# A reciprocal square root without its Newton step on VectorE, and a row of ones made by ScalarE

## The chip, the cores and the metric

The kernel runs on one core of a Trainium2 chip. The metric is the device time of one execution in microseconds (us). A core has five engines with their own queues: TensorE (PE, with its weight loads shown as PEld), VectorE (DVE), ScalarE (ACT), GpSimd (POOL) and SyncE (SP), which issues the DMA transfers here. Each engine works through its instructions in order and waits for others on semaphores.

## What is computed

Four images of 56 x 56 pixels and 96 channels pass through four layers. Layers 0 and 1 contain a selective scan (a state-space recurrence) in four directions over the image, with 192 inner channels and 16 states; layers 2 and 3 are an attention without softmax, followed by a feed-forward part with quantized weights and activations (fp8 products, fp16 sums). In front of the parts and between them stand normalisations:

```python
def layer_norm(x, w, b, eps=1e-06):
    m = jnp.mean(x, axis=-1, keepdims=True)
    v = jnp.mean((x - m) ** 2, axis=-1, keepdims=True)
    return (x - m) * jax.lax.rsqrt(v + eps) * w + b
...
h = da_t * h + db_t * x_t[..., None]
y_t = jnp.einsum('bds,bs->bd', h, c_t)
```

The attention is linear in its values, so the kernel needs only the Gram matrix of the normalised tokens, each extended by a one (for the biases): a matrix of 97 x 97 per image.

## The kernel before

**The scan.** The two scan layers are one long sequence of rounds: 2 layers x 4 images x 4 directions x 7 chunks of 448 tokens x 2 halves of the channels x 4 groups of states = 1792 rounds. Each round takes three tiles of 128 x 448 (`NG = 3`). `decay` (L640) lets ScalarE compute exp(dt * a) into one PSUM tile `da` for each of the three; `begin` (L645) lets TensorE spread b over the partitions into PSUM (L580); VectorE multiplies du by b (L673), for two of the three tiles, or all three in the rounds in `OWN` and `OWN_TAIL`, where GpSimd does not take the third (L651). VectorE then runs three scans (L699), ScalarE saves and restores the carries (L703, L658), GpSimd multiplies the result by c (L709, `hc`), and TensorE adds up over the states (L737). The parts of the next chunk (softplus, L489 and L490; products on GpSimd, L496 and L593) are woven in at fixed rounds.

**The rest, beside the scan.** The other work runs in lanes beside the scan: `load`, `middle`, `fuse`, `attend`, Python generators that issue one step at a time. The scan loop yields twice a round: once as slot "F", after the multiplies have been issued, and once as slot "C", between the first and the second of the three scans. So what a lane issues in a C slot stands in VectorE's queue between scan 0 and scan 1, and in ScalarE's queue behind the first decay of the next round. A lane's yield names the slot that its next step wants, the PSUM tiles that it holds, and the load in us that it puts on ScalarE (`a`) and TensorE (`p`); `overlap` (L902) and `room` (L940) admit steps by these numbers. Inside the scan the order of the instructions on TensorE, ScalarE, VectorE and GpSimd is that of the calls (`manual_schedule`, L1303). While image i of layer 1 is scanned, image i-1 goes through `fuse` and `attend`; the last image does so in a tail without a scan, after `late` (L191), with more buffers and an order that is left to the scheduler. Before the scan, `load(0)` runs alone; in it `self.tables` is still false.

**The normalisations.** `normed` (L814) centres x by a matmul (`factor`), squares it on ScalarE (L776) and calls `spread_factor` (L779). That averages the squares by four small matmuls into a PSUM tile `ps` of 112 x 4 (L789), turns the variances into 1/sqrt, and spreads the four columns over 96 partitions by four matmuls (L809), whose result VectorE multiplies with x in a later C slot (L823, L1125, L1166; through a copy at L1111 and L1117). The 1/sqrt takes two forms. With `tables` false: a GpSimd power (L794). Otherwise, in the F slot, Ln and Exp(-0.5 x) on ScalarE (L801, L802) give a first value r; in the next C slot three VectorE instructions do one Newton step on it (L804 to L806). `spread_factor` in this second form runs 245 times: 21 in `load`, 56 in `middle`, 84 in `fuse` with the `gram` it calls, and 84 in `attend` with its `gram`.

**The row of ones.** `gram` (L1216) takes a tile `xra` of 97 x 448, one of three buffers inside the scan (`depth`) and of six in the tail, fills row 96 with ones (L1220), lets `normed` write rows 0 to 95, stores these by DMA (L1222), transposes all 97 rows on TensorE (L1226) and adds up the Gram matrix. It is called 56 times, 28 from `fuse` and 28 from `attend`. The row is issued in the C slot (or behind a yield of C) from which `gram` is entered.

Of the kernel before, what the change touches and what calls it, by code (L numbers as in the profile page):

```python
# [11 lines left out]
F32 = mybir.dt.float32  # L12
# [3 lines left out]
AF = mybir.ActivationFunctionType  # L16
ALU = mybir.AluOpType
# [5 lines left out]
C = 96  # L23
# [5 lines left out]
NT = 112  # L29
CW = 448  # L30
# [134 lines left out]
class Net:  # L165
# [613 lines left out]
    def spread_factor(self, eps, *terms):  # L779

        nc = self.nc
        ps = self.ps()
        blocks = [slice(q * NT, (q + 1) * NT) for q in range(4)]
        for q, b in enumerate(blocks):
            for n, (sq, avg) in enumerate(terms):
                nc.tensor.matmul(ps[:NT, q : q + 1], sq[:, b], avg, start=n == 0, stop=n == len(terms) - 1)  # L789
        rs = self.wp.tile([NT, 4], F32, name="rs", bufs=12)  # L790
        if not self.tables:
            yield "F0 a.3"
            nc.scalar.activation(rs, ps[:NT, :4], AF.Identity, bias=self.eps[eps][:NT])
            nc.gpsimd.tensor_tensor(rs, rs, self.power[:NT], ALU.pow)  # L794
            yield "C1 p2.4"
        else:

            yield "F1 a.6"

            r, t = self.wp.tile([NT, 4], F32, name="rs", bufs=12), ps[:NT, 4:8]  # L800
            nc.scalar.activation(r, ps[:NT, :4], AF.Ln, bias=self.eps[eps][:NT])  # L801
            nc.scalar.activation(r, r, AF.Exp, scale=-0.5)  # L802
            yield "C1 p2.4"
            nc.vector.scalar_tensor_tensor(t, ps[:NT, :4], eps, r, ALU.add, ALU.mult)  # L804
            nc.vector.scalar_tensor_tensor(t, t, -0.5, r, ALU.mult, ALU.mult)
            nc.vector.scalar_tensor_tensor(rs, t, 1.5, r, ALU.add, ALU.mult)  # L806
        ps = self.ps()[:C, :CW]
        for q, b in enumerate(blocks):
            nc.tensor.matmul(  # L809
                ps[:, b], rs[:, q : q + 1].to_broadcast([NT, C]), self.ident[:NT, :NT], start=True, stop=True  # L810
            )
        return ps
# [403 lines left out]
    def gram(self, n, i, c, x, s):  # L1216

        nc = self.nc
        xr = self.wp.tile([C + 1, CW], F32, name="xra", bufs=self.depth)
        nc.vector.memset(xr[C : C + 1], 1.0)  # L1220
        yield from self.normed(1e-5, x, 1, xr[:C])
        nc.sync.dma_start(self.xrd[i][:, s], xr[:C])  # L1222
        m = C + 1
        ps = self.ps()
        for q in range(4):
            nc.tensor.transpose(ps[:NT, q * m : (q + 1) * m], xr[:, q * NT : (q + 1) * NT], self.ident[:m, :m])  # L1226
        yield "F0 a.5"
        t = self.w()
        nc.scalar.copy(t[:NT, : 4 * m], ps[:NT, : 4 * m])
        yield "C1 p2.4"  # L1230
        ps = self.ps()[:m, :m]
        for q in range(4):
            a = t[:NT, q * m : (q + 1) * m]
            nc.tensor.matmul(ps, a, a, start=q == 0, stop=q == 3)
        yield "C0"
        if c == 0:
            self.g[i] = self.wp.tile([m, m], F32, name="gram", bufs=3)
            nc.vector.tensor_copy(self.g[i], ps)
        else:
            nc.vector.tensor_tensor(self.g[i], self.g[i], ps, ALU.add)  # L1240
# [98 lines left out]
```

## Time and profile before

Three runs took 8621.33, 8633.8 and 8647.61 us, median 8633.8 us. The profiled execution has a span of 8626.1 us and a mean granted TensorE clock of 0.892.

| engine | busy us | share of the span | instructions |
|---|---|---|---|
| DVE | 7939.4 | 92% | 10933 |
| POOL | 7594.3 | 88% | 4075 |
| PE | 7475.5 | 87% | 33459 |
| ACT | 5909.3 | 69% | 12541 |

| group | count | busy us | mean ns |
|---|---|---|---|
| L699 DVE scans | 5376 | 5523.8 | 1072 |
| L673 DVE multiplies | 4172 | 2330.0 | 605 |
| L709 POOL multiply by c | 1792 | 5168.2 | 2885 |
| L651 POOL third multiply | 1204 | 1374.6 | 1142 |
| L643 ACT decays | 5376 | 3394.5 | 633 |
| L804 / L805 / L806 DVE, with `ps` as their PSUM tile | 215 each | 34.4 / 36.6 / 34.7 | 160 / 170 / 161 |
| L1220 DVE memset of the row | 56 | 24.2 | 432 |

A group's busy time is the union of its instructions, its mean the length of one; where instructions overlap, the two differ. The remaining 30 of the 245 Newton steps have their PSUM tile in `da`, `y`, `b` or `pp`, in the tail. Busy shares over the whole span mix three stages: up to about 119 us the lead-in, up to 8286 us the scan, then the tail.

### The profile page before, as it was taken

How to read it: one execution, taken by the hardware profiler on the slowest of the kernel's cores; microseconds unless marked ns; L12 is line 12 of the kernel's file. 1: busy time of each engine (PE TensorE's matmuls, PEld its weight loads, DVE VectorE, ACT ScalarE, POOL GpSimd, SP SyncE). 2: the span in 40 equal slices, each digit the busy share in tenths (PEclk: the TensorE clock that was granted, in tenths of full speed). 3: DMA queues.
4: the chain of work that ended last, by engine and by line, in shares of the span. 5: the costliest groups of instructions: out<-in, count | busy, mean ns of one | idle time of the engine just before them, and what ended most of it. 6: DMA issues, size and time to landing. Idle time of an engine off the chain costs nothing. (4 is left out here: it accounts for less than half of the span.)

```text
span 8626.1 us, 120872 instructions
## 1 busy us (share of the span) xinstructions
PE 7475.5 (87%) x33459; PEld 2708.0 (31%) x33459; DVE 7939.4 (92%) x10933; ACT 5909.3 (69%) x12541; POOL 7594.3 (88%) x4075
## 2 busy tenths in 40 slices
PE   6788888898889888898889989988899888998997
PEld 3222223232333223232223223323233232333345
DVE  5999999999999999999999999999999999999951
ACT  5777667676777667776677756667766777667646
POOL 4888989999999999999999999999999999999940
PEclk8888889898999989998899989988899888998987
DMA  5677677677777777776777777667776677766731
GB/s 144 159 184 174 164 179 179 162 167 166 187 169 179 168 185 173 172 176 159 185 175 171 170 174 166 161 154 167 185 174 150 161 165 186 171 149 163 168 90 45
DMA packets 951340, 1417.89 MB, mean 164 GB/s; under 512 B 176578, under 2 KB 943812, under 8 KB 949796
## 3 DMA queue, kind: packets, MB, share of 16 engines
q1 hardware_dynamic: 949888, 1408.37, 68.6%
q8 instruction: 263, 4.31, 0.2%
q14 instruction: 417, 3.42, 0.2%
q10 hardware_dynamic: 772, 1.80, 0.1%
HBM read 1141.42 MB, written 268.14 MB: 163 GB/s over the span
## 5 line engine op out<-in xcount | busy, mean ns | idle before, releaser
L709 POOL TENSOR_TENSOR hc<-v,cb 128x1344 f32<-128x1344 f32 x1792 | 5168.2, 2885 | 499.4 <-DVE v L699 288.1
L699 DVE TENSOR_TENSOR_SCAN v<-da,v 128x449 f32<-128x449 f32 (+1 forms) x5376 | 5523.8, 1072 | 60.4 <-ACT v L658 33.2
L643 ACT ACTIVATE da<-dt,na 128x448 f32<-128x448 f32 x5376 | 3394.5, 633 | 1583.2 <-DVE v L699 1557.3
L673 DVE TENSOR_TENSOR v<-du,b 128x448 f32<-128x448 f32 x4172 | 2330.0, 605 | 136.5 <-PE b L580 50.0
L737 PE MATMUL y<-hc,four 128*32 128x448 f32 x14336 | 1959.6, 622 | 4.3 <-POOL hc L709 4.3
L580 PE MATMUL b<-cf,sel 128*128 128x448 bf16 x1792 | 682.6, 381 | 954.7 <-DVE v L673 949.9
L651 POOL TENSOR_TENSOR v<-du,cb 128x448 f32<-128x448 f32 x1204 | 1374.6, 1142 | 95.8 <-DMA cb<-cd 69.0
L724 PE MATMUL y<-w,zeros 128*96 128x448 bf16 x5117 | 1441.9, 399 | 0.0
L724 PEld LDWEIGHTS <-zeros 128*96 128x96 bf16 x5117 | 631.5, 134 | 1306.5 <-issue 1149.6
L737 PEld LDWEIGHTS y<-hc,four 128*32 128x32 f32 x14336 | 297.5, 114 | 1291.2 <-issue 917.7
L428 PE MATMUL pp<-U,wd 96*128 96x448 f32 x896 | 671.3, 836 | 9.1 <-DMA U<-u 9.1
L733 PE MATMUL y<-Y,ident 96*96 96x448 f32 x672 | 539.8, 892 | 42.3 <-ACT Y L744 23.6
L496 POOL TENSOR_TENSOR duc<-dtc,U 96x448 f32<-96x448 f32 x448 | 559.8, 1250 | 4.6 <-ACT dtc L490 4.6
L886 PE MATMUL ps<-win,dg 64*64 64x220 f32 (+9 forms) x1962 | 509.3, 454 | 0.0
L703 ACT COPY carry<-v 128x3 f32<-128x3 f32 x1536 | 299.2, 195 | 287.7 <-DVE v L699 286.9
L480 PE MATMUL pp<-cf,wd 12*96 12x448 f32 (+1 forms) x896 | 488.0, 627 | 1.1 <-ACT cf L467 1.0
L489 ACT ACTIVATE dtc<-pp,wd 96x448 f32<-96x448 f32 x448 | 279.3, 623 | 270.1 <-PE pp L480 267.7
L593 POOL TENSOR_TENSOR cf<-cf 64x448 f32<-64x448 f32 x448 | 417.5, 932 | 35.7 <-ACT cf L467 0.6
L744 ACT COPY Y<-y 96x448 f32<-96x448 f32 x448 | 339.3, 757 | 31.8 <-PE y L737 30.6
L886 PEld LDWEIGHTS ps<-win,dg 64*64 64x64 f32 (+2 forms) x1962 | 230.6, 158 | 329.9 <-issue 272.7
L580 PEld LDWEIGHTS <-sel 128*128 128x128 bf16 x1792 | 186.7, 104 | 350.2 <-issue 285.8
L733 PEld LDWEIGHTS y<-Y,ident 96*96 96x96 f32 x672 | 116.8, 184 | 553.2 <-ACT da L643 243.8
(426 smaller groups left out, 6066.0 us busy)
## 6 DMA issues: line engine op xcount, KB each, us to landing
cb<-cd SPq DMA_DIRECT2D x3584, 112.0 KB, 4.3
dt<-dd SPq DMA_DIRECT2D x1792, 168.0 KB, 4.4
du<-dd SPq DMA_DIRECT2D x1792, 168.0 KB, 4.2
dd<-dtc SPq DMA_DIRECT2D x448, 168.0 KB, 2.0
dd<-duc SPq DMA_DIRECT2D x448, 168.0 KB, 2.1
U<-u SPq DMA_DIRECT2D x112, 168.0 KB, 4.6
z<-w SPq DMA_DIRECT2D x56, 224.0 KB, 3.1
u<-w SPq DMA_DIRECT2D x56, 224.0 KB, 3.4
```

Source lines behind the costliest of these rows:

```text
L428: self.nc.tensor.matmul(ch.ps.rearrange("p (a b) -> p a b", b=HS), ch.par.wx[:, e], self.in_order(self.U[e], ch.orient, ch.c * CS, CS), st ...
L496: self.nc.gpsimd.tensor_tensor(du.rearrange("p (a b) -> p a b", b=HS), ch.dtc[e].rearrange("p (a b) -> p a b", b=HS), self.in_order(self.U ...
L580: self.nc.tensor.matmul(ps, self.sel[:, q], self.upper(ch.cf), start=True, stop=True)
L643: nc.scalar.activation(da[g][:, TOKENS], ch.dt[e][:, g], AF.Exp, scale=ch.par.na[:, e, q, g : g + 1])
L651: nc.gpsimd.tensor_tensor(v[:, 2, TOKENS], ch.du[e][:, 2], ch.cb[q][:, 1], ALU.mult)
L673: nc.vector.tensor_tensor(v[:, g, TOKENS], ch.du[e][:, g], b, ALU.mult)
L699: nc.vector.tensor_tensor_scan(v[:, g, way], da[g][:, way], v[:, g, way], 0.0, ALU.mult, ALU.add)
L709: nc.gpsimd.tensor_tensor(hc, v[:, :, TOKENS], ch.cb[q][:, 0].unsqueeze(1).to_broadcast([128, NG, CS]), ALU.mult)
L724: self.nc.tensor.matmul(self.y[:C], self.zeros, self.some, start=False, stop=False)
L733: nc.tensor.matmul(o, w, self.in_order(a, ch.orient, ch.c * CS, CS), start=True, stop=False)
L737: nc.tensor.matmul(self.y[32 * n : 32 * n + 32], self.four, hc[:, g], start=n == 3, stop=n == 3 or q == NQ - 1,)
L886: self.nc.tensor.matmul(o[:, a - r0 : e - r0, x0:x1], diag[:, tap], win[:, a + dy - lo : e + dy - lo, x0 + dx : x1 + dx], start=n == 0, st ...
```

## The change

Two edits.

The Newton step goes. Ln and Exp now write straight into `rs`, the tile that the broadcast matmuls read; the second tile r and the spare columns of the PSUM tile are not used any more. This drops three small VectorE instructions per use. Only the form with `tables` true is touched.

The row of ones in `gram` is made by ScalarE: an activation Copy with scale 0 and bias 1 of a column of the identity matrix, broadcast over 448 elements, takes the place of a VectorE memset. It stands at the same point of the program. The numbers in the yields stay as they are.

```diff
             yield "F1 a.6"
-
-            r, t = self.wp.tile([NT, 4], F32, name="rs", bufs=12), ps[:NT, 4:8]
-            nc.scalar.activation(r, ps[:NT, :4], AF.Ln, bias=self.eps[eps][:NT])
-            nc.scalar.activation(r, r, AF.Exp, scale=-0.5)
+            nc.scalar.activation(rs, ps[:NT, :4], AF.Ln, bias=self.eps[eps][:NT])
+            nc.scalar.activation(rs, rs, AF.Exp, scale=-0.5)
             yield "C1 p2.4"
-            nc.vector.scalar_tensor_tensor(t, ps[:NT, :4], eps, r, ALU.add, ALU.mult)
-            nc.vector.scalar_tensor_tensor(t, t, -0.5, r, ALU.mult, ALU.mult)
-            nc.vector.scalar_tensor_tensor(rs, t, 1.5, r, ALU.add, ALU.mult)
...
         xr = self.wp.tile([C + 1, CW], F32, name="xra", bufs=self.depth)
-        nc.vector.memset(xr[C : C + 1], 1.0)
+        nc.scalar.activation(xr[C:], self.ident[C : C + 1, :1].to_broadcast([1, CW]), AF.Copy, scale=0.0, bias=1.0)
         yield from self.normed(1e-5, x, 1, xr[:C])
```

## The prediction

> **What bounds the kernel now.** I first cut the span into its stages with the busy time of each engine per stretch: a lead-in up to 119 us, eight passes of the scan of about 1021 us each (119 to 8286 us, two layers by four images), and a tail of 340 us. The rows are passes 0, 3 and 6; columns after the length are PE, PEld, DVE, ACT, POOL busy, granted PE clock, DMA share.
>
> ```profile
> core 0: us, PE busy (x) PEld busy (x) DVE busy (x) ACT busy (x) POOL busy (x), PEclk, DMA share, GB/s
> 119.00:1140.00 1021.00, 836.60 (x3624) 281.19 (x3624) 957.14 (x1274) 727.84 (x1486) 903.74 (x470) 0.86 0.71 170
> ...
> 3182.00:4203.00 1021.00, 881.30 (x3932) 297.76 (x3933) 988.18 (x1303) 718.05 (x1469) 953.94 (x505) 0.91 0.74 175
> ...
> 6245.00:7265.00 1020.00, 911.18 (x4190) 335.46 (x4189) 982.74 (x1387) 704.31 (x1591) 951.78 (x518) 0.90 0.70 166
> ...
> sum 8167.00, PE 7108.32 PEld 2484.96 DVE 7847.36 ACT 5686.54 POOL 7553.74; mean PE 888.54 PEld 310.62 DVE 980.92 ACT 710.82 POOL 944.22
> ```
>
> DVE is busy 7847 of 8167 us (96%), POOL 92%, PE 87%, ACT 70%. So who waits for whom decides. These are rows of the view of waits for passes 5 to 7 (5224 to 8286 us); the figures are us in total, times, longest.
>
> ```profile
> DVE ps L804 <- ACT rs L802: 42.9, 53, 2.4
> DVE w L1100 <- ACT w L776: 8.8, 7, 3.9
> ...
> POOL hc L709 <- DVE v L699: 103.9, 126, 4.6
> ...
> PE b L580 <- DVE v L673: 270.3, 272, 2.7
> ...
> ACT da L643 <- DVE v L699: 542.0, 710, 2.7
> ```
>
> POOL, PE and ACT all wait for DVE; DVE itself waits for little, and its longest wait in these passes is that of the first Newton instruction (L804) for Exp on ACT (L802). DVE sets the end of the scan, POOL is close behind. The tail has DVE busy 72 of 340 us; its chain runs over PE and ACT.
>
> Third, DVE in order of time, to see what the edited lines cost where they stand (start us, length us). Scan instructions (L699) without anything between them start (3.05 - 1.08)/2 = 0.985 us apart.
>
> ```profile
> 5311.19 0.17 DVE L804 SCALAR_TENSOR_TENSOR ps<-ps,rs 112x4 f32<-112x4 f32 x1 [0.22 <-ACT rs L802]
> ...
> 5328.76 1.08 DVE L699 TENSOR_TENSOR_SCAN v<-da,v 128x449 f32<-128x449 f32 x1
> 5329.76 0.15 DVE L804 SCALAR_TENSOR_TENSOR ps<-ps,rs 112x4 f32<-112x4 f32 x1
> 5329.94 0.17 DVE L805 SCALAR_TENSOR_TENSOR ps<-ps,rs 112x4 f32<-112x4 f32 x1
> 5330.15 0.16 DVE L806 SCALAR_TENSOR_TENSOR rs<-ps,rs 112x4 f32<-112x4 f32 x1
> 5330.23 1.08 DVE L699 TENSOR_TENSOR_SCAN v<-da,v 128x449 f32<-128x449 f32 x1
> ...
> 5338.86 3.05 DVE L699 TENSOR_TENSOR_SCAN v<-da,v 128x449 f32<-128x449 f32 x3
> ...
> 5342.87 1.08 DVE L699 TENSOR_TENSOR_SCAN v<-da,v 128x449 f32<-128x449 f32 x1
> 5344.10 0.43 DVE L1220 MEMSET xra<- 1x448 f32 x1
> 5344.56 1.09 DVE L699 TENSOR_TENSOR_SCAN v<-da,v 128x449 f32<-128x449 f32 x1
> ```
>
> A Newton trio pushes the next scan from 0.985 to 1.47 us: it costs 0.485 us without a wait. A memset of the row pushes it to 1.69 us: 0.705 us, though it is listed with 0.43 us, since it starts 0.25 us late.
>
> **What the Trainium skill says.** "VectorE: DVE Perf Modes", section "Two Vector instructions with no wait between them": an instruction whose output starts in another quadrant than the last output into the same memory waits until all earlier Vector instructions have finished. The row lies at partition 96, the scan's output at 0. The trace agrees: no overlap ahead of the memset or behind it, 0.705 instead of 0.43 us. "ScalarE: Activation LUTs", section "Table sets: the hidden batching unit": copy is in every set, and Ln and Exp share one. The trace agrees for Copy (the cf copies of L467 have no table load); for Ln and Exp it does from about 320 us on, while the first three uses at L801 and L802 each have a load of 1.28 us. These uses stay, so the number of loads does not change. "SBUF — State Buffer", section "SBUF: two separate sides": DVE and POOL exclude each other only over a shared port pair, used by DVE instructions with two SBUF inputs or in a two-port mode. The trace shows POOL's hc multiply between 2855 and 2948 ns over the whole run, beside any DVE work, so I expect no change in POOL's durations.
>
> **The change, part by part.**
> *Newton trios.* 245 run, 205 of them in the scan: 21 in pass 0, 56 in passes 1 to 4, 128 in passes 5 to 7. 205 x 0.485 = 99 us of DVE. With them goes DVE's wait for L802: 73.7 us in the scan (42.9 in passes 5 to 7, about 7 in 1 to 4, 23.6 in pass 0).
> *Memsets.* 44 in the scan, all in passes 5 to 7: 44 x 0.705 = 31 us of DVE.
> *What DVE gains*: 99 + 74 + 31 = 204 us: 136 in passes 5 to 7 (62 + 43 + 31), 34 in passes 1 to 4 (27 + 7), 34 in pass 0 (10 + 24).
> *The wait that moves.* The broadcast matmuls (L809) now wait for ACT's Exp itself instead of the trio. Behind them on PE stand the y sums and the next b spread (L580), which DVE needs. PE waited for the trio only 3.5 us in passes 5 to 7, and Exp ends before the trio did, so PE starts earlier: cost nothing. The PSUM tile comes free at Ln instead of at L806, also earlier.
> *The row on ACT.* No 1x448 activation is in the trace. Nearest row: SBUF to SBUF, 96x448, L490, 577 ns; the page on ScalarE, section "What ACT_TABLE_LOAD costs", prices immediate scale and bias at 186 ns + 0.833 ns per element, which I estimate as 559 ns; the bottom is the pitch of PSUM copies, 0.42 us. I take 0.56: 44 x 0.56 = 25 us of ACT in the scan. It is queued in the C slot, behind the first decay (L643) and its carry copy, ahead of the second decay. DVE needs that second decay after two more scans, two multiplies and a scan, 2.0 + 1.1 + 1.0 = 4.1 us; ACT needs 0.64 + 0.18 + 0.56 + 0.63 = 2.0 us. Hidden, if ACT is not already late. The row's buffer is one of three, and the memset had to wait for its release 1.5 us in all, once; ACT inherits that.
> *What the others take back.* In passes 5 to 7 POOL waits only 104 us for DVE's scans, less than the 136 us DVE gains. Once that is used up POOL gates, and POOL and DVE are coupled by three v buffers. PE has 270 us and is not first. I take some 90% of the 104: 95 us. In passes 1 to 4 POOL and PE have room (POOL waits over 20 us per pass for scans): 29 of 34. In pass 0 the three L804 waits with table loads in them make 8.9 us; after the one at 275 us ACT still has two loads to do before the decay that DVE needs at 280.0, so that one is not won, and PE runs at 0.86 clock: 22 of 34. Scan: 95 + 29 + 22 = 146 us.
> *Tail.* 40 trios leave a DVE that is idle four fifths of the time; a trio lies on the chain at 8543.56 to 8544.14, 0.6 us, so perhaps 2 to 5 us are won, while 12 rows add 12 x 0.56 = 7 us to ACT, half of it hidden. I put zero, plus or minus 10, since the order of the tail is not written by hand.
> Sum: 8634 - 146 = 8488 us.
>
> **Rivals.**
> 1. *DVE's whole gain comes through* (0.08): POOL's other waits (on y sums, on L809: 38 us in passes 5 to 7) shrink too. For: those stand behind PE work that starts earlier now. Against: POOL would be busy 98% there. 8634 - 204 - 5 = 8425.
> 2. *POOL and PE become the bound in passes 5 to 7* (0.18): coupling through three buffers and more DVE waits for b leave a third of the gain there, 45, and 35 in the others. For: POOL's multiplies come in groups in rounds 5 to 7 of a chunk, where POOL has no idle time. Against: in rounds with a trio POOL waits for DVE up to 1.3 us. 8634 - 80 = 8554.
> 3. *ACT becomes the gate, slower than before* (0.06): ACT waits in order for the row's buffer, and the decays stand behind it. If each of 44 rows cost a round of about 4.55 us plus 0.56, that is 225 us against the 204 won: 8634 + 21 = 8655. For: DVE waited for ACT at L804 53 times there, so ACT does run late. Against: the buffer was free in all cases but one, and ACT idles 542 us on scans in these passes.
> 4. *No difference* (0.04): the freed time becomes waits for b, since PE takes a lower granted clock. PE at 911 of 1020 us would need 0.90 to fall to 0.84.
>
> **How the numbers follow.** My forecast has 0.64. The range 8425 to 8570 holds it with its spread (8450 to 8525), rival 1 and rival 2 with some 16 us of scatter; what lies outside is rivals 3 and 4 and the edges. Within 0.3% is 8608 to 8660. Faster: 0.64 + 0.08 + 0.18 = 0.90; same 0.05; slower 0.05 (rival 3 lies near the border and is shared between the two).
>
> **What would show it.** DVE busy in the scan falls by about 130 us (205 trios, 44 memsets), with no row for L804 to L806; DVE's list of waits has no L804, and no other row grows by more than some 20 us. POOL's wait for scans in passes 5 to 7 falls from 104 to about 20 and its share rises above 96%. Pass 6 is about 32 us shorter, passes 1 to 4 about 7 each. L809 waits for ACT rs by a few us. ACT shows 56 short rows of 0.4 to 0.6 us, and a wait there for DMA or PE stays under 5 us. I am wrong if DVE's waits for b, v of POOL, or da grow by tens of us, if the granted clock falls, or if ACT is seen waiting at the row.

## The result, and the profile after

The changed kernel takes 8486.6 us in the median, against 8640.7 us for the kernel before in the same comparison: a ratio of 0.9828, 95% interval 0.98 to 0.9855 (about 24 us either way). The forecast was 8488 us.

The profiled execution after has a span of 8506.0 us; it is the slowest of those timed, some 20 us above the median, so stage lengths read from it give away some of the gain. The busy time of each engine by stage (passes 0 to 4, passes 5 to 7, tail; the borders between passes are taken at the start of the same instruction, L463, in both kernels; columns as in the prediction), first before, then after:

```profile
core 0: us, PE busy (x) PEld busy (x) DVE busy (x) ACT busy (x) POOL busy (x), PEclk, DMA share, GB/s
118.00:5129.00 5011.00, 4277.77 (x18946) 1438.60 (x18946) 4812.00 (x6343) 3543.11 (x7227) 4621.69 (x2438) 0.90 0.73 172
5129.00:8286.00 3157.00, 2830.55 (x12976) 1046.36 (x12974) 3036.30 (x4284) 2143.59 (x4843) 2932.05 (x1593) 0.90 0.70 166
8286.00:8626.00 340.00, 287.57 (x1293) 177.75 (x1291) 72.12 (x223) 173.42 (x397) 28.02 (x25) 0.78 0.17 47
```

```profile
119.00:5079.00 4960.00, 4260.05 (x18936) 1436.61 (x18936) 4779.47 (x6110) 3536.76 (x7228) 4619.20 (x2438) 0.90 0.73 174
5079.00:8158.00 3079.00, 2801.99 (x12987) 1039.47 (x12985) 2963.04 (x3857) 2162.69 (x4887) 2929.33 (x1593) 0.91 0.71 170
8158.00:8506.00 348.00, 298.86 (x1293) 184.72 (x1291) 48.78 (x91) 179.75 (x409) 27.93 (x25) 0.75 0.17 45
```

The scan lost 51 us in passes 0 to 4 and 78 us in passes 5 to 7; the tail grew by 8. In the scan VectorE's busy time fell by 32.5 + 73.3 = 106 us and its idle time by only 23 us. Yet the wait at L804, 73.7 us, is gone, so about 50 us of idle time are new (more, counting the short gaps around trios and memsets). The view of waits says where in passes 5 to 7 (total us, times, longest), first two rows of before, then after:

```profile
DVE v L673 <- PE b L580: 3.4, 5, 1.7
...
DVE xq L1166 <- PE ps L809: 1.0, 1, 1.0
```

```profile
DVE v L673 <- issue: 18.3, 16, 3.6
DVE w L1095 <- ACT w L776: 17.9, 12, 6.2
DVE v L673 <- PE b L580: 17.9, 20, 2.6
DVE w L1112 <- PE ps L1110: 9.1, 9, 1.8
DVE xq L1161 <- PE ps L804: 9.1, 8, 2.8
DVE v L699 <- POOL v L651: 7.7, 10, 1.9
DVE xra L818 <- PE ps L804: 6.5, 10, 1.9
...
POOL hc L709 <- DVE v L699: 67.4, 70, 5.2
...
PE b L580 <- DVE v L673: 233.2, 219, 3.3
```

Added up by the engine waited for, VectorE's waits in these passes were before: ACT 62, PE 23, POOL 13, without a releaser 5; after: ACT 32, PE 50, POOL 14, without a releaser 18. VectorE's waits for GpSimd did not grow. The rise is at TensorE: the b spread (3.4 to 17.9 us) and the products that read the spread factor (L1161 and L818, before L1166 and L823: 1.7 to 15.6 us). The 13 us more without a releaser stand at the multiplies (L673), and the profile names no cause for them. GpSimd still waits 67 us for scans. In passes 0 to 4 the row that grew most (from 0.4 us) is again a product that reads the spread:

```profile
DVE w L818 <- PE ps L804: 20.0, 14, 3.1
```

One such place, in order of time on VectorE and on TensorE:

```profile
8140.99 1.08 DVE L699 TENSOR_TENSOR_SCAN v<-da,v 128x449 f32<-128x449 f32 x1
8143.59 0.62 DVE L1161 TENSOR_TENSOR xq<-w,ps 96x448 fp8e5<-96x448 f32 x1 [1.52 <-PE ps L804]
8144.13 1.08 DVE L699 TENSOR_TENSOR_SCAN v<-da,v 128x449 f32<-128x449 f32 x1
...
8140.30 2.48 PE L881 MATMUL ps<-win,dg 96*96 96x448 f32 x6
8142.62 0.93 PE L804 MATMUL ps<-ident,rs 112*96 112x112 f32 x8
```

VectorE is ready at 8142.07, but TensorE has a piece of a convolution (L881) ahead of the spread and delivers it at 8143.55. What stands ahead differs from place to place: of the 35.6 us in which VectorE waits for a spread in the scan, 17 us are behind matmuls of other steps beside the scan (L840 and L988), 8 us behind a projection of a later chunk (L428), and a convolution is ahead at this one place only.

The row on ScalarE was estimated at 0.56 us and takes 0.571, and ScalarE never waits at it in the scan:

```profile
L1215 ACT ACTIVATE xra<-ident x44: 571/571/573, 5255.0 to 8080.9; 1x448 f32<-1x448 f32 x44
```

### The profile page after: what moved, and what is told of

Same layout as the page of the kernel before. It is cut to its first block, busy times and chain, and to the rows that moved or that the text cites. A ratio compares the mean times of both kernels' runs of the same rounds, so it can differ in the third digit from the quotient of the medians.

```text
span 8506.0 us, 120303 instructions
## 1 busy us (share of the span) xinstructions
PE 7442.0 (87%) x33459; PEld 2707.3 (32%) x33459; DVE 7810.2 (92%) x10142; ACT 5928.4 (70%) x12597; POOL 7589.0 (89%) x4075
## 5 line engine op out<-in xcount | busy, mean ns | idle before, releaser
L673 DVE TENSOR_TENSOR v<-du,b 128x448 f32<-128x448 f32 x4172 | 2331.4, 605 | 164.7 <-PE b L580 68.4
L737 PE MATMUL y<-hc,four 128*32 128x448 f32 x14336 | 1942.7, 617 | 3.7 <-POOL hc L709 3.6
L428 PE MATMUL pp<-U,wd 96*128 96x448 f32 x896 | 671.2, 836 | 13.7 <-DMA U<-u 13.7
L737 PEld LDWEIGHTS y<-hc,four 128*32 128x32 f32 x14336 | 297.0, 114 | 1206.0 <-issue 816.8
L881 PE MATMUL ps<-win,dg 64*64 64x220 f32 (+9 forms) x1962 | 507.9, 453 | 0.0
L881 PEld LDWEIGHTS ps<-win,dg 64*64 64x64 f32 (+2 forms) x1962 | 229.7, 158 | 326.2 <-issue 267.4
```

What stands on the lines that cost most here:

```text
L428: self.nc.tensor.matmul(ch.ps.rearrange("p (a b) -> p a b", b=HS), ch.par.wx[:, e], self.in_order(self.U[e], ch.orient, ch.c * CS, CS), st ...
L673: nc.vector.tensor_tensor(v[:, g, TOKENS], ch.du[e][:, g], b, ALU.mult)
L737: nc.tensor.matmul(self.y[32 * n : 32 * n + 32], self.four, hc[:, g], start=n == 3, stop=n == 3 or q == NQ - 1,)
L881: self.nc.tensor.matmul(o[:, a - r0 : e - r0, x0:x1], diag[:, tap], win[:, a + dy - lo : e + dy - lo, x0 + dx : x1 + dx], start=n == 0, st ...
```

## Experiments

**The two edits apart.** The Newton step alone is taken away:

```diff
-        nc.scalar.activation(xr[C:], self.ident[C : C + 1, :1].to_broadcast([1, CW]), AF.Copy, scale=0.0, bias=1.0)
+        nc.vector.memset(xr[C : C + 1], 1.0)
```

> The first edit alone: the three Newton instructions are gone, the row of ones stays a VectorE memset. Theory (VectorE sets the end, the parts add up, most of what it gains comes through): the memsets are 44 x 0.705 = 31 us of VectorE in the scan, so this lies 20 to 31 us above the full change, at 8507 to 8518 us. Rival (the row on ScalarE delays the decays as much as the memset cost VectorE): same as the full change, 8487 us, or below.

Measured: 8518.2 us, ratio 0.9867 (0.9852 to 0.9882). As the theory has it: with the step gone, the memsets cost 32 us in the medians (34 by the ratios), against 31 worked out. The interval of the full change overlaps with this one; that of the kernel below in which nobody makes the row, at 8489.5 us, does not.

The row alone moves to ScalarE, with the kernel before otherwise as it was (the reverse edit):

> The second edit alone: the row of ones by ScalarE, the Newton step kept. Theory: 20 to 31 us below the kernel before, 8610 to 8621 us, and no wait of ScalarE at the row. Rival (ScalarE is late in these passes, and the row makes the wait of L804 for Exp longer): 8641 us or more, with the wait at L804 in passes 5 to 7 grown from 43 us.

Measured: 8656.4 us against 8640.1, ratio 1.0026 (1.0014 to 1.0037): slower, as the rival said. The waits of VectorE in passes 5 to 7 (of an execution that took 14 us more than the median):

```profile
DVE ps L804 <- ACT rs L802: 52.9, 57, 2.4
DVE v L673 <- issue: 15.6, 14, 2.5
DVE w L1100 <- ACT w L776: 15.1, 9, 5.6
```

The wait at L804 grew from 42.9 to 52.9 us, the wait for squares at L1100 from 8.8 to 15.1; VectorE's waits for ACT together from 62 to 81. So the same edit is worth 32 to 34 us with the step gone and costs 22 us with it. The next two runs ask which half of the edit does that.

**The row made by nobody.** Three constant tiles take turns inside the scan, and their row 96 is written once; in the tail the row is made as it was. First on the full change:

```diff
+        xra = [const.tile([C + 1, CW], F32, name=f"xra{j}") for j in range(DEPTH)]
+        for t in xra:
+            nc.vector.memset(t[C : C + 1], 1.0)
+        self.xra = cycle(xra)
...
+        if self.ring is None:
+            xr = next(self.xra)
+        else:
+            xr = self.wp.tile([C + 1, CW], F32, name="xra", bufs=self.depth)
```

> The full change, but inside the scan the row of ones is written only once into three constant tiles that take turns, so neither VectorE nor ScalarE makes it there (in the tail ScalarE still does). Theory (the 44 activations of 0.57 us are hidden on ScalarE): same as the full change, 8480 to 8490 us. Rival (they delay the decays and squares that VectorE waits for): up to 25 us below, 8462 us.

Measured: 8489.5 us, ratio 0.9831 (0.9818 to 0.9845), the same as the full change. Without the step the row on ScalarE is hidden, to within the intervals.

The same on the kernel before, Newton step kept:

> The kernel before, its Newton step kept, with the rows of ones written only once inside the scan: the 44 memsets are gone and ScalarE has nothing for them. It tells why moving the row alone was 16 us slower (8656) although it freed 31 us of VectorE. Theory (with the step kept, VectorE waits at L804 for ScalarE, and 0.57 us more on ScalarE come straight back there): 20 to 31 us below the kernel before, 8609 to 8621 us. Rival (as long as VectorE stops at L804 for Exp, what it gains just before is waited out there, whoever makes the row): 8640 to 8656 us.

Measured: 8629.1 against 8635.7 us, ratio 0.9996 (0.9987 to 1.0005), so 31 us less work on VectorE won at most 11. Neither figure was met; it lies between the two, and the wait at the step's first instruction, which has line 808 in this kernel, had grown from 42.9 to 49.5 us, though ScalarE had nothing more to do:

```profile
DVE ps L808 <- ACT rs L806: 49.5, 54, 3.7
DVE w L1104 <- ACT w L780: 15.3, 9, 7.0
```

In this one execution the scan was some 17 us shorter than before and the tail 14 us longer; the tails of the profiled executions lie between 336 and 361 us, the next experiment's apart. So in the scan about half of the 31 us was kept, and how much came back at the step, and how much only in the tail, isn't settled. The six kernels, as the difference to the kernel before (ratio less one, times 8636 us; the intervals are 8 to 13 us either way, for -149 it is 24):

| | row by VectorE | row by nobody | row by ScalarE |
|---|---|---|---|
| step kept | 0 | -3 | +22 |
| step gone | -115 | -146 | -149 |

Reading along the lines: with the step kept, 44 rows of 0.57 us = 25 us on ScalarE show in full (from -3 to +22); with the step gone they show not at all. The explanation that offers itself is that VectorE stops for Exp there, so that ScalarE's lateness becomes its own. It is not shown: between the kernels with the row by nobody and by ScalarE the wait at the step grew only from 49.5 to 52.9 us and the one for squares not at all (15.3 and 15.1), while passes 5 to 7 grew by some 31 us (3140 to 3171). The rest lies in many small waits, the largest part of it (4.1 to 15.6) without a releaser.

**The step later, to take away its wait only.** On the kernel before:

```diff
+            yield "C1"
             yield "C1 p2.4"
             nc.vector.scalar_tensor_tensor(t, ps[:NT, :4], eps, r, ALU.add, ALU.mult)
```

> The kernel before with the Newton step moved one C slot later, so that Exp is long done when VectorE comes to it: the same work, without the wait of 74 us. Theory (the wait costs what it shows): 50 to 74 us below the kernel before, 8567 to 8591 us. Rival (ScalarE and TensorE are late at that point anyway, and VectorE will stand a little further on instead): 8625 to 8641 us, with waits of VectorE for b (L580) or da (L643) grown by tens of us.

Measured: 8693.6 us, ratio 1.0066 (1.0053 to 1.0079): outside both. The wait at L804 was gone from the list, and the scan was 14 us shorter in the profile (its last scan ended at 8272 us against 8286), but the tail took 425 us instead of 340: one more slot in each normalisation made the lanes too long for their passes, and work that belongs beside the scan ran after it (1536 matmuls in the tail instead of 1293). What the wait is worth can't be read from this run, but its profile has the rival's sign: over the scan VectorE's wait for b rose from 50 to 73 us. And it shows that a slot in a lane has a price here.

**The step kept as work, unused.** On the full change, in the same slot, with a constant for r:

```diff
+            d, t, h = self.wp.tile([NT, 4], F32, name="rs", bufs=12), ps[:NT, 4:8], self.power[:NT]
+            nc.vector.scalar_tensor_tensor(t, ps[:NT, :4], eps, h, ALU.add, ALU.mult)
+            nc.vector.scalar_tensor_tensor(t, t, -0.5, h, ALU.mult, ALU.mult)
+            nc.vector.scalar_tensor_tensor(d, t, 1.5, h, ALU.add, ALU.mult)
```

> The full change plus three VectorE instructions of the Newton step's shapes at its place, with a constant in the place of r and their result used by nothing: VectorE's work of the step is back (205 x 0.485 = 99 us in the scan), its wait for Exp is not. Theory (work and wait each cost about what the profile shows): 60 to 99 us above the full change, 8547 to 8586 us; the rest up to the kernel with only the row moved, 8656 us, is the wait. Rival (the wait was free, VectorE would have waited for something else): 8630 us or more.

Measured: 8600.6 us, ratio 0.9963 (0.9951 to 0.9976), 114 us above the full change: more than the 99 us of work, and outside both figures. The waits in passes 5 to 7 say why (L803 is the first of the three, L799 is Ln):

```profile
DVE ps L803 <- ACT rs L799: 37.5, 42, 3.3
DVE w L1099 <- ACT w L776: 16.9, 10, 6.8
```

The wait for Exp was to be gone, but one for Ln has taken its place, probably because the three instructions write into spare columns of the PSUM tile that Ln reads. So the run did not separate work from wait: the 114 us hold both. What it leaves is some 55 us between the kernel with only the row moved (8656) and this one, in which VectorE does not need Exp and the spread on TensorE does not stand behind VectorE. How the step's share splits into work and wait stays open.

**Who takes back: GpSimd?** One third multiply per chunk is moved in passes 5 to 7, first to VectorE, then to GpSimd:

```diff
-OWN_TAIL = (3, 4)
+OWN_TAIL = (3, 4, 6)
```

> The full change with one third multiply per chunk handed from GpSimd to VectorE in passes 5 to 7 (84 in all): GpSimd has 84 x 1.09 = 92 us less, VectorE 84 x 0.56 = 47 us more. Theory (VectorE is still the bound, with TensorE behind it): 30 to 47 us above the full change, 8517 to 8534 us. Rival (GpSimd has become the bound there): same or faster, 8450 to 8490 us.

Measured: 8541.7 us, ratio 0.9893 (0.9878 to 0.9909), 55 us above the full change, a little more than the work moved to VectorE (47) and than the theory's range.

```diff
-OWN_TAIL = (3, 4)
+OWN_TAIL = (4,)
```

> The opposite: one more third multiply per chunk on GpSimd in passes 5 to 7, VectorE has 47 us less, GpSimd 92 us more, of the 150 us in which it is idle there. Theory (VectorE is still the bound): 10 to 35 us below the full change, 8452 to 8477 us. Rival (GpSimd has become the bound): 20 to 70 us above, 8507 to 8557 us.

Measured: 8534.6 us, ratio 0.9886 (0.9872 to 0.9899), 48 us above: the theory failed here and the rival's range was met. The waits in passes 5 to 7, first with less, then with more on GpSimd:

```profile
POOL hc L709 <- DVE v L699: 155.7, 164, 4.6
...
DVE v L673 <- PE b L580: 16.6, 23, 2.0
DVE v L699 <- POOL v L651: 8.8, 8, 2.7
```

```profile
DVE v L699 <- POOL v L651: 58.1, 96, 1.7
DVE v L673 <- PE b L580: 45.9, 45, 5.3
...
POOL hc L709 <- DVE v L699: 40.8, 39, 4.3
```

With GpSimd relieved by 92 us VectorE's waits stay as they were (8.8 for GpSimd, 16.6 for b), so no wait for GpSimd was there to be won in the changed kernel. With 92 us more there is: VectorE waits 58 us for it. One multiply per chunk either way is a loss, so neither engine alone is the bound there: they are balanced to within that step. The finer step, in every second chunk of passes 0 to 4:

```diff
-            ahead = NQ * e + q not in (OWN_TAIL if ch.l and ch.i else OWN)
+            ahead = NQ * e + q not in (OWN_TAIL if ch.step % 2 or ch.l and ch.i else OWN)
```

> The full change with one third multiply moved from VectorE to GpSimd in every second chunk of passes 0 to 4 (GpSimd 15 us more per pass, of the 68 us in which it is idle there; VectorE 8 us less). Theory (VectorE alone is the bound in those passes): 10 to 40 us below the full change, 8447 to 8477 us. Rival (the two are balanced, as passes 5 to 7 turned out to be, where moving one either way cost 48 to 55 us): 8490 to 8510 us.

Measured: 8489.8 us, ratio 0.983 (0.9815 to 0.9844): no difference, at the lower edge of the rival. This step is too small to win or lose anything there.

**Who takes back: TensorE's load?** The convolutions with three taps, six left out:

```diff
-            for ps, r0, rows in parts:
+            for ps, r0, rows in parts if n < 3 else ():
...
-                    start=n == 0, stop=n == 8,
+                    start=n == 0, stop=n == 2,
```

> The full change with TensorE relieved and nothing else moved: the depthwise convolutions (in the passes 1 to 4 and 5 to 7) run only 3 of their 9 taps, at the same slots; six taps are left out, so the result differs. Theory (in the scan it is TensorE that takes back what VectorE gained: VectorE's waits for PE rose from 23 to 50 us in passes 5 to 7): 30 to 60 us below the full change, 8427 to 8457 us, and VectorE's waits for PE in passes 5 to 7 down to 20 to 30 us. Rival (GpSimd takes it back, as forecast): 8480 to 8490 us, since GpSimd's work is the same.

Measured: 8489.2 us, ratio 0.9837 (0.9824 to 0.9851): nothing won, which is the rival's figure. And with fewer of the zero matmuls:

```diff
-WARM, PER_P = 7.3, 1.6
+WARM, PER_P = 5.5, 1.6
```

> The full change with fewer of the zero matmuls that only keep TensorE busy (WARM 5.5 instead of 7.3), so TensorE has some 50 us less to do in each pass, in nearly every round. Theory (the waits of VectorE for PE, 47 us in passes 5 to 7, come from TensorE being behind with its queue): these waits at most 25 us and 20 to 50 us off the full change, 8437 to 8467 us. Rival (they come from the length of the chain squares, average, Ln, Exp, spread, product, at a granted clock that falls when there is less to do, as with three taps, where it fell from 0.895 to 0.872 and nothing was won): 8487 us or more, with the waits for PE at 45 us or more.

Measured: 8489.0 us, ratio 0.9835 (0.9819 to 0.9851): nothing won either, again as the rival said. Passes 5 to 7 of the two, three taps first:

```profile
5068.00:8146.00 3078.00, 2745.30 (x12686) 1004.53 (x12685) 2959.86 (x3856) 2161.94 (x4884) 2928.29 (x1593) 0.89 0.72 170
```

```profile
5064.00:8138.00 3074.00, 2741.74 (x12432) 996.07 (x12428) 2959.60 (x3855) 2160.09 (x4886) 2927.15 (x1593) 0.89 0.71 170
```

TensorE was busy some 60 us less, at a granted clock of 0.89 instead of 0.91 (0.872 and 0.868 over the span against 0.895), and VectorE's waits for it stayed, 51 us with three taps and 56 us with less fill. So less busy time of TensorE in all did not shorten VectorE's waits for it; a relief at an unchanged clock could not be had this way. Both runs took work from other places than those that count: a convolution stood ahead of a spread only once, and the zero matmuls that were left out come ahead of the b spread, not between it and the spread factor.

**Who takes back: the order in TensorE's queue?** The steps of one slot in order of their TensorE work:

```diff
-                    chosen.append((act, len(chosen), g))
-            for act, n_, g in sorted(chosen):
+                    chosen.append((act, pe, len(chosen), g))
+            for act, pe, n_, g in sorted(chosen):
```

> The full change, and within one C slot the steps with less TensorE work are issued first, so that the spread matmuls (L804) stand ahead of a convolution piece instead of behind it; the work is the same. Theory (VectorE's waits for PE, 36 us of them at L804 in the whole scan, come from what stands ahead of the spread in TensorE's queue): the waits at L804 at most 12 us in the scan and 10 to 35 us off the full change, 8452 to 8477 us. Rival (they come from the length of the chain, or return as waits for b): 8480 to 8495 us.

Measured: 8515.3 us, ratio 0.986 (0.9844 to 0.9877), 29 us slower than the full change. The waits at the spread rose in passes 5 to 7 from 15.6 to 22.5 us, and in passes 0 to 4 from 20.0 to 28.1:

```profile
DVE xq L1161 <- PE ps L804: 14.9, 9, 3.3
...
DVE xra L818 <- PE ps L804: 7.6, 11, 0.8
```

This does not clear the order, because the edit did the opposite of what it was meant to do. The spread counts as 2.4 us of TensorE work in its yield; many other steps count less (0.6 to 1.9) and now go ahead of it. In the timeline matmuls of other steps beside the scan stand between the b spread and the spread in 37 of the 193 rounds of the scan that hold a spread, before the change as after it, and in 71 in this run; the one convolution stayed where it was. The same place with the full change, and in this run:

```profile
6825.36 0.96 PE L737 MATMUL y<-hc,four 128*32 128x448 f32 x8
6826.25 1.01 PE L804 MATMUL ps<-ident,rs 112*96 112x112 f32 x8
6827.10 0.92 PE L1149 MATMUL ps<-w,wq 96*96 96x448 f32 x2
...
6827.30 0.62 DVE L1161 TENSOR_TENSOR xq<-w,ps 96x448 fp8e5<-96x448 f32 x1 [0.37 <-PE ps L804]
```

```profile
6830.59 1.72 PE L737 MATMUL y<-hc,four 128*32 128x448 f32 x8
6832.24 1.81 PE L1149 MATMUL ps<-w,wq 96*96 96x448 f32 x2
6833.84 1.18 PE L804 MATMUL ps<-ident,rs 112*96 112x112 f32 x8
...
6835.06 0.62 DVE L1161 TENSOR_TENSOR xq<-w,ps 96x448 fp8e5<-96x448 f32 x1 [3.33 <-PE ps L804]
```

With the product L1149 ahead of the spread instead of behind it, VectorE's wait went from 0.37 to 3.33 us: some 1.8 of the 3 us are L1149 itself, the rest are matmuls that ran longer at this place (the y sums 1.72 instead of 0.96). So what stands ahead of the spread in TensorE's queue does lengthen these waits. In passes 5 to 7 TensorE's own waits list none at L804: it has the data and comes late through its queue. That the order was the same before the change and the waits were not fits a VectorE that now comes to the product earlier. Whether an order with the spread first would win the 36 us was not tried.

No version faster than the changed kernel was found; rows once, the half move, three taps and less fill are equal to it within the intervals.

## Why the prediction was right, point by point

- *VectorE sets the end of the scan*: right for the kernel before. Taking the step and the memsets away brought 149 us by the ratio, and moving 47 us of work to VectorE afterwards cost 55. After the change GpSimd is level with it in passes 5 to 7: taking 47 us off VectorE by giving GpSimd 92 lost 48.
- *The memset costs 0.705 us, not the 0.43 us listed*: right with the step gone, 29 to 34 us measured for 31. But the sum treated the edits as independent, and they aren't: with the step kept, taking the memsets away won 3 us (at most 11). The order in which the two are credited changes their shares from -115 and -34 to +22 and -171.
- *The trios cost 0.485 us each*: VectorE's busy time fell by 106 us in the scan, of which 44 x 0.43 = 19 us are memsets; the list said about 130 in all. In passes 0 to 4, where there are no memsets, it fell by 32.5 us for 77 trios, 0.42 us each. Work and wait together brought 115 us when taken away alone, of the 173 us that the sum put down as VectorE's gain; their separate shares weren't measured.
- *The row on ScalarE is hidden*: right, and shown: none at all is as fast. Hidden holds only without the step; with it the same 25 us show in full.
- *The wait moves to TensorE at no cost*: this step failed. VectorE's waits for TensorE rose by 28 us in passes 5 to 7 (23 to 50) and by 24 us in passes 0 to 4 (54 to 78). Those for ScalarE fell by 30 us in each (L804 had had 42.9 and 30.8; in passes 5 to 7 the wait for squares took 9 of that back). So nearly as much as VectorE no longer waited for ScalarE, it waited for TensorE. The prediction looked at how long TensorE had waited for the trio, 3.5 us, and not at what stands between the b spread and the spread in TensorE's queue, which is what a VectorE that comes earlier runs into. Its sign of being wrong, a row that grows by tens of us, did not show it either: no row grew by more than 20 us, only their sum did.
- *What the others take back*: the size was about right and the engine wrong, so that the sum came within 2 us of the measured time is in part luck. Forecast were savings of 22, 29 and 95 us in pass 0, passes 1 to 4 and passes 5 to 7; the profiled execution gives 27, 24 and 78, an execution at the median some 20 us more in all. But GpSimd was named as the one that takes it back, with its wait for scans down to about 20 us; it fell only from 104 to 67, and relieving GpSimd won nothing. Of the 204 us listed as VectorE's gain, 50 to 55 did not come; the waits for TensorE grew by 28 + 24 = 52, though VectorE's busy time, too, fell by less than was listed.
- *Tail*: zero plus or minus 10 was forecast, 8 us more in the one profiled execution. The 12 rows on ScalarE there are 12 x 0.57 = 7 us, but kernels whose tail is the same differ by 14 us there, so this is no confirmation.
- *The rivals*: GpSimd as bound is refuted for this kernel, though one more multiply per chunk makes it true. ScalarE as gate didn't come in the full change. Moving the row alone did make the kernel slower, but not by the route that the rival named: ScalarE never waited for the row's buffer in the scan. The granted clock didn't fall (0.892 to 0.895); the figure of 0.84 in that rival does not come out of its own numbers, since 911 us at 0.90 fill 1020 us only at 0.80.

## What to carry to other kernels

A small instruction on the engine that sets the end costs its work, its place in the queue, and the coupling that its operand brings. Two such edits need not add up: moving the row was worth some 33 us with the step gone and cost 22 us with it, so don't judge one half of such a change alone. Why the step makes that difference is argued here, not shown.

Where several engines are above 87% busy, expect part of a gain to come back as waits spread over the neighbours. The list of waits added up by the engine waited for shows at whom. Taking work from that engine won nothing here; what stood ahead of the late instruction in its queue, read place by place, told more. And an edit of an order is only a test of that order once the timeline shows that the order came out as meant.

## What was not expected of the hardware

- Taking work from TensorE lowered its granted clock: 0.895 to 0.872 with six taps fewer, to 0.868 with about a third fewer zero matmuls. The y sums (L737) then took 628 to 631 ns in the mean of passes 5 to 7, instead of 616.
- A 1x448 activation of one partition took 571 ns, as long as 96x448 (577 ns at L490). On VectorE a memset of one row at partition 96 cost 0.705 us of the queue for 0.43 us of work.
